# Sorting grouped edge quads in halves of 256, with on-chip copies that bring the rows together again

## The chip, the cores and the metric

The kernel runs on one core of a Trainium2 chip. The metric is device time in microseconds (us), the median of several runs. A core has five engines that run side by side: TensorE (PE, matmuls), VectorE (DVE), ScalarE (ACT), GpSimd (POOL, here the issuer of scatters to device memory) and SyncE (SP, the issuer of loads, stores and copies). Each engine takes its instructions in order; semaphores tie them together. All transfers run on the same 16 DMA engines.

## The reference

One layer of a graph network: 6250 nodes with 128 features and 200,000 edges, sorted by `dst`. Every edge takes the projected row of its `dst` node, multiplies it by a filter that a small network makes from 20 edge features, and adds the product to the row of its `src` node; `src` is random.

```python
h = jnp.maximum(_layernorm(x, axis=-1), 0.0)                  # passed on as atomic_embedding
idx_i = pair_indices[0]                                       # src
idx_j = pair_indices[1]                                       # dst
x = atomic_embedding @ W_in
W_ij = shifted_softplus(f_ij @ W_f1 + b_f1) @ W_f2 + b_f2
W_ij = W_ij * f_ij_cutoff
x_ij = x[idx_j] * W_ij
out = jax.ops.segment_sum(x_ij, idx_i, num_segments=N_ATOMS)
return shifted_softplus(out @ W_o1 + b_o1) @ W_o2 + b_o2      # the caller adds its x
```

## The kernel before, in words

The edges are cut into 391 quads of 512 (four chunks of 128). The main loop (`for i in range(...)`, with `s1_`, `s2_`, `s3_` stages and the hook points `run(i, ...)`) works on several quads at once, each stage one to four iterations behind the one before. For every quad PE makes the filter (`z` L363, `W` L562) and gathers the node rows (`xg` L554), ACT scales them (`xc` L567), and DVE multiplies (`s2_m`, L577). What remains is the sum into the `src` rows, and there are two ways for it:

- A *listed* quad (200 of the 391 go this way or the plain way at the start) gives its product `s` to POOL, which scatters it in four indirect DMAs of 128 rows (`scatter`, L639) with addition into one of four tables `acc` in device memory. `acc_of` rotates the tables, so a scatter waits until the one before it on the same table has landed.
- A *grouped* quad (`sorted_quads`: 191 quads, every second one from 8 on) is summed on PE. Its `src` nodes fall into 16 groups of 392 (`GN`). `rank_*` gives each of 32 chunks' edges its rank within its group and so a slot; `perm_oh` (L719) builds a one-hot matrix `pm` of 128 edges x 576 slots per chunk; `permute` (L744) multiplies it with the three bfloat16 parts of the product (`pt`, 387 columns with two index columns), four blocks of 128 slots (4 groups x 32 slots each), each the sum over four chunks; `perm_out` (L750, ACT) casts a block into `mst`. Edges beyond a group's 32 slots go to 64 overflow slots, which `over_pe` (L757) sorts for two quads into one block of 128 rows; they are summed and scattered by the `over_*` steps, one scatter for a pair of quads.

Eight grouped quads make a round. Four *units* per round then sum the sorted rows: `unit_oh` (L825, DVE) makes one-hots of the local node number, `unit_pe` (L840) multiplies 32-row bands of `mst` with them (four bands beside each other), and `unit_evac` (L851) adds the result to `accT` on chip. `unit_slots` sets the iterations of the units: from `ULAG` iterations after a round's last quad on, at iterations that `UCLASSES` allows, and `mbufs` counts how many `mst` buffers that takes.

The order is written out by hand: `AT` gives each step its distance in iterations from its quad and its hook point (for example `"p0": (3, "PE2")`), `put` and `at` enter it, `clear` moves it off the iterations that hold units. The order of the code is the order on each engine. SP issues, per pair of quads, three `ft` loads (L345), two `rb` loads (L349), a register load (L351) and four `wn` loads (L356), beside the `sb` loads (L394) and the rewriting of the edge features (`fb` L313, `fsd` L335); each waits for a free buffer and for the SP transfer eight before it to land.

After the loop the three remaining tables are loaded, added to `accT` and passed through the output network.

Of the kernel before, what the change touches and what calls it, by code (L numbers as in the profile page):

```python
# [20 lines left out]
P = 128  # L21
# [3 lines left out]
CAP = 32  # L25
OVC = 64
SLOTS = GRP * CAP + OVC
MP0 = 8
# [3 lines left out]
RKQ = 8  # L32
ULAG = 5
AT = {
# [40 lines left out]
def tile_gnn(ctx: ExitStack, tc: tile.TileContext, x, fB, cT, srcT, srcr, srci, dstr, win_, wf1, wf2, bias, bo1c, wo1,  # L75
# [29 lines left out]
    units = {i for us in uslots for i in us}  # L105
    mbufs = [max(len(qs) + sum(q > qs[-1] and (q + 3 if q + 4 in units else q + 4 + s // 2) <= us[s] for q in mpq) for qs, us in zip(rounds, uslots))
             for s in range(4)]
    splain = [q for q in range(NQ) if q not in mpi]
# [292 lines left out]
    def s1_eq(q):  # L401
        if not plainq(q):
            return
        n = plain[q]
        eq = wk.tile([P, 4, P], F32, tag="eq", name="eq", bufs=2)
# [262 lines left out]

    def before_me(ps_t, src, w, own=False):
        n = src.shape[1]  # L670
        nc.tensor.matmul(ps_t, trib if own else tri, src, start=True, stop=False)
        o = ps_t.rearrange("p (j c) -> p j c", c=4 * w)
        v = src.rearrange("p (j c) -> p j c", c=4 * w)
        for k in range(1, 4):
            nc.tensor.matmul(o[:, :, k * w:], onesb, v[:, :, :(4 - k) * w], start=False, stop=(k == 3))

    def rank_count(r):
        n = rk[r]["n"]
        t = ps.tile([P, 512], F32, tag="B", name="rkp", bufs=4)
        before_me(t[:, :n * GRP], rk[r]["G"].rearrange("p x g -> p (x g)"), GRP, own=True)  # L680
        rk[r]["ps"] = t

    def rank_own(r):
        n = rk[r]["n"]
        rank = wk.tile([P, 4 * RKQ], F32, tag="rank", name="rank", bufs=1)[:, :n]
        nc.vector.tensor_reduce(rank, rk[r]["ps"][:, :n * GRP].rearrange("p (x g) -> p x g", g=GRP), axis=AX.X,  # L686
                                op=ALU.max)
        ov = wk.tile([P, 4 * RKQ], BF16, tag="ov", name="ov", bufs=1)[:, :n]
        nc.vector.tensor_scalar(ov, rank, float(BIG + CAP), None, op0=ALU.is_ge)
        rk[r]["rank"], rk[r]["ov"] = rank, ov  # L690

    def rank_over(r):
        t = ps.tile([P, 512], F32, tag="B", name="rko", bufs=4)
        before_me(t[:, :rk[r]["n"]], rk[r]["ov"], 1)
        rk[r]["po"] = t

    def rank_slot(r):
# [3 lines left out]
        a = wk.tile([P, 4 * RKQ], F32, tag="ra", name="ra", bufs=1)[:, :n]  # L701
        nc.vector.scalar_tensor_tensor(a, rk[r]["cnt"], float(CAP), rk[r]["rank"], op0=ALU.mult, op1=ALU.add)
        t = wk.tile([P, 4 * RKQ], F32, tag="rt", name="rt", bufs=1)
        tn = t[:, :n]
        nc.vector.scalar_tensor_tensor(tn, po, float(BIG + GRP * CAP), a, op0=ALU.add, op1=ALU.subtract)
        nc.vector.tensor_tensor(tn, tn, ov, op=ALU.mult)
# [33 lines left out]

    def permute(q, s):
        t = ps.tile([P, 512], F32, tag="B", name="pq", bufs=4)
        for c in range(4):
            nc.tensor.matmul(t[:, :PW], mp[q]["pm"][:, c, s * P:(s + 1) * P], high(mp[q]["pt"][:, c:c + 1, :PW])[:, 0],  # L744
                             start=(c == 0), stop=(c == 3))
        mp[q]["q", s] = t

    def perm_out(q, s):
        mp[q]["ms", s] = wk.tile([P, MW], BF16, tag=f"ms{s}", name="mst", bufs=mbufs[s])
        nc.scalar.copy(mp[q]["ms", s][:, :PW], mp[q].pop(("q", s))[:, :PW])  # L750

    def over_pe(q):
        qs = mpq[mpi[q] // 2 * 2:mpi[q] + 1]
        t = ps.tile([P, 512], F32, tag="B", name="po", bufs=4)
        for c in range(4):
            for h, p in enumerate(qs):
                nc.tensor.matmul(t[h * OVC:(h + 1) * OVC, :PW], mp[p]["pm"][:, c, GRP * CAP:],  # L757
                                 high(mp[p]["pt"][:, c:c + 1, :PW])[:, 0], start=(c == 0), stop=(c == 3))
        mp[q]["po"] = t, len(qs) * OVC

    def over_out(q):
        t, n = mp[q].pop("po")
        mo = mos[mpi[q] // 2 % 2]
        nc.scalar.copy(mo[:n, :PW], t[:n, :PW])
        if n < P:
            nc.vector.memset(mo[n:, :PW], 0.0)

# [52 lines left out]
    def unit_oh(r, s, h):  # L820
        qs = rounds[r]
        for q in qs[h * len(qs) // 3:(h + 1) * len(qs) // 3]:
            so = wk.tile([P, GN], BF16, tag="so", name="so", bufs=RND + 1)
            w = mp[q]["ms", s].bitcast(F32)
            nc.vector.tensor_scalar(so, iotw[:, :GN], w[:, 3 * P // 2:3 * P // 2 + 1], None, op0=ALU.is_equal)  # L825
# [4 lines left out]
    def unit_pe(r, s):  # L830
# [5 lines left out]
        for q in qs:  # L836
            for k in range(3):
                for g in range(4):
                    v = slice(g * CAP, (g + 1) * CAP)
                    nc.tensor.matmul(ts[g][:, :GN], mp[q]["ms", s][v, k * P:(k + 1) * P], mp[q]["oh"][v],  # L840
                                     start=(q == qs[0] and k == 0), stop=(q == qs[-1] and k == 2))
# [53 lines left out]
    with tc.manual_schedule():  # L895
# [266 lines left out]
        def x_load(k):  # L1162
            tag, n = (("pt", 3), ("pt", 3), ("pm", 2), ("pm", 2))[k]
            t_ = pg.tile([P, PW, 4] if tag == "pt" else [P, 4, SLOTS // 2], F32, tag=tag, name="xl")
            v = t_.rearrange("p a b -> p (a b)")
# [98 lines left out]
        for q in mpq:  # L1264
# [135 lines left out]
    with tc.For_i(0, redo, 1):  # L1400
# [8 lines left out]
        with tc.For_i(0, trips, 1) as ci:  # L1409
# [50 lines left out]
            nc.vector.scalar_tensor_tensor(m[:, :P], W, ok[:, 3:4], xw, op0=ALU.mult, op1=ALU.mult)  # L1460
            eq = wk.tile([P, P], F32, tag="eq", name="feq", bufs=2)
            nc.vector.tensor_tensor(eq, sb, scol.to_broadcast([P, P]), op=ALU.is_equal)
# [282 lines left out]
```

## Time and profile before

| | |
|---|---|
| median of 3 runs | 1913.39 us (1912.6 to 1916.29) |
| the profiled execution | 1913.11 us |
| its span, first to last instruction | 1911.3 us |
| mean granted TensorE clock | 0.979 |
| bytes moved by DMA | 267.55 MB in 351575 packets |

How to read the profile: "busy" is the time in which an engine executes; issues of DMAs by SP are not counted as busy. A group row names the line, engine, operation, `out<-in` tiles, shapes and count, then busy us and mean ns of one, then the idle time of the engine just before these instructions and what ended it ("issue" is waiting for nothing that the profile shows). A timeline row has start, length, instruction and, in brackets, the idle time before. PEld is PE's weight load, which overlaps its matmuls; matmuls are pipelined, so their mean length is longer than the busy time each takes.

### The profile page before, as it was taken

The page shows a single profiled execution, that of the slowest core. Times are in us where ns is not written, and L with a number is a line of the kernel's source. Part 1 is how long each engine was busy: PE and PEld are TensorE (multiplying, and loading weights), DVE is VectorE, ACT ScalarE, POOL GpSimd, SP SyncE. Part 2 cuts the span into 40 slices and gives each one's busy share as a digit, 9 for nine tenths or more (in the row PEclk, how much of TensorE's full clock was granted, in tenths as well). Part 3 has the DMA queues.
Part 4 walks back from the last instruction along what each step waited for, and adds up shares of the span by engine and source line. Part 5 has one row for each costly group of instructions (what it writes and reads, how often), then busy time and mean ns, then how long its engine had stood idle before and what let it go on. Part 6 is the DMA issues. An engine that isn't in the chain of part 4 may idle for free. (4 is left out here: it accounts for less than half of the span.)

```text
span 1911.3 us, 58065 instructions
## 1 busy us (share of the span) xinstructions
PE 1809.2 (95%) x20601; PEld 1228.2 (64%) x20601; DVE 1655.9 (87%) x4692; ACT 1474.9 (77%) x4045; POOL 1509.0 (79%) x961
## 2 busy tenths in 40 slices
PE   4679999999999999999999999999999999999986
PEld 3556666666666666666666666666666666666654
DVE  5678998899999989999999889889889888888767
ACT  4569788878887878878887787787787787787725
POOL 4578777788888888887777888888888888878755
PEclk8789999999999999999999999999999999999998
DMA  8788777767776777776776667677676667666648
GB/s 287 201 208 167 142 162 135 131 125 131 139 135 123 131 126 130 129 152 116 125 135 126 124 126 129 118 129 129 116 130 129 116 130 127 117 117 133 106 99 269
DMA packets 351575, 267.55 MB, mean 140 GB/s; under 512 B 96655, under 2 KB 315194, under 8 KB 351282
## 3 DMA queue, kind: packets, MB, share of 16 engines
q1 hardware_dynamic: 218516, 197.56, 35.9%
q0 software_dynamic: 132208, 66.05, 34.6%
q8 instruction: 162, 2.65, 0.6%
q14 instruction: 131, 1.07, 0.2%
q10 hardware_dynamic: 558, 0.20, 0.0%
HBM read 154.65 MB, written 109.00 MB: 138 GB/s over the span
## 5 line engine op out<-in xcount | busy, mean ns | idle before, releaser
L639 POOL DMA_INDIRECT acc<-s,lji x751 | 1201.5, 1600 | 267.9 <-issue 174.4
L744 PE MATMUL pq<-pt,pm 128*128 128x387 bf16 x3056 | 583.2, 337 | 1.2 <-ACT s L597 0.6
L567 ACT ACTIVATE xc<-xg,cb 128x128 f32<-128x128 f32 x1564 | 448.1, 376 | 171.5 <-PE xg L554 151.9
L750 ACT CAST mst<-pq 128x387 bf16<-128x387 f32 x764 | 364.0, 487 | 91.7 <-PE pq L744 68.1
L562 PEld LDWEIGHTS W<-w,a 128*128 128x128 f32 x3128 | 421.7, 196 | 17.9 <-issue 7.3
L744 PEld LDWEIGHTS <-pm 128*128 128x128 bf16 x3056 | 294.4, 98 | 197.5 <-issue 4.9
L840 PE MATMUL un<-so,mst 32*128 32x392 bf16 x9168 | 411.3, 325 | 10.0 <-DVE rank L686 2.8
L562 PE MATMUL W<-w,a 128*128 128x128 f32 x3128 | 420.1, 278 | 0.0
L840 PEld LDWEIGHTS <-mst 32*128 32x128 bf16 x9168 | 249.8, 93 | 146.7 <-issue 19.0
L373 ACT ACTIVATE a<-a,con 128x512 f32<-128x512 f32 x391 | 282.5, 723 | 11.6
L733 DVE TENSOR_TENSOR pt<-pt 128x512 f32<-128x512 f32 x382 | 261.0, 683 | 0.0
L719 DVE TENSOR_SCALAR pm<-iotp,pos 128x576 bf16<-128x576 f16 x764 | 255.6, 396 | 0.0
L368 ACT ACTIVATE a<-z 128x512 f32<-128x512 f32 x391 | 236.6, 605 | 5.9 <-PE z L363 5.9
L851 DVE TENSOR_TENSOR accT<-un,accT 128x392 f32<-128x392 f32 x368 | 182.4, 558 | 63.1 <-PE un L840 34.8
L639 POOL DMA_INDIRECT acc<-os,oji x108 | 180.9, 1675 | 51.3 <-issue 12.9
L825 DVE TENSOR_SCALAR so<-iot,mst 128x392 bf16<-128x392 f16 x764 | 215.3, 333 | 2.2 <-PE un L840 1.9
L577 DVE TENSOR_TENSOR pt<-W,xc 128x512 f32<-128x512 f32 x191 | 131.6, 689 | 57.0 <-ACT xc L567 23.9
L363 PE MATMUL z<-ft,ws 123*128 123x512 bf16 x391 | 153.8, 394 | 19.9 <-POOL b2rep L979 8.4
L554 PE MATMUL xg<-wn,oh 63*128 63x128 bf16 x1564 | 156.6, 221 | 13.5 <-DVE oh L380 12.1
L577 DVE TENSOR_TENSOR s<-W,xc 128x512 f32<-128x512 f32 x188 | 128.7, 685 | 45.5 <-ACT xc L567 34.8
L551 PE MATMUL W<-b2rep,onesb 64*128 64x512 bf16 x391 | 152.9, 391 | 0.0
L639 POOL DMA_INDIRECT acc<-s,ji x48 | 81.0, 1688 | 42.1 <-DMA acc<-s,ji 20.5
(215 smaller groups left out, 1796.0 us busy)
## 6 DMA issues: line engine op xcount, KB each, us to landing
rb<-reld SPq DMA_DIRECT2D x391, 64.0 KB
sb<-src SPq DMA_DIRECT2D x192, 128.0 KB
fsd<-f SPq DMA_DIRECT2D x49, 480.0 KB
ft<-fsd SPq DMA_DIRECT2D x195, 120.0 KB
fb<-in_fB_dram SPq DMA_DIRECT2D x49, 320.0 KB
ft<-fsd SPq DMA_DIRECT2D x195, 80.0 KB
wn<-tab SPq DMA_DIRECT2D x782, 15.8 KB
acc<-s,lji POOLq DMA_INDIRECT x751
```

The source lines that it names most:

```text
L368: nc.scalar.activation(a, st[q]["z"], AF.Exp)
L373: nc.scalar.activation(a, a, AF.Ln, bias=half, scale=0.5)
L562: nc.tensor.matmul(W[:, c, :], st[q]["a"][:, c * P:(c + 1) * P], w2, start=False, stop=(c == 3))
L567: nc.scalar.mul(xc[:, c, :], st[q]["xg"][:, c, :], late["c", q // CQ][:, 4 * (q % CQ) + c:4 * (q % CQ) + c + 1])
L577: nc.vector.tensor_tensor(m[:, :, :P], st[q]["W"], st[q]["xc"], op=ALU.mult)
L639: nc.gpsimd.indirect_dma_start(out=accs[k][:rows, :], out_offset=bass.IndirectOffsetOnAxis(ap=ji, axis=0), in_=s, in_offset=None, compute_ ...
L719: nc.vector.tensor_scalar(pm[:, c], iotp, rk[r]["pos"][:, 4 * j + c:4 * j + c + 1], None, op0=ALU.is_equal)
L733: nc.vector.tensor_tensor(pt[:, :, k * P:(k + 1) * P], a, high(a), op=ALU.subtract)
L744: nc.tensor.matmul(t[:, :PW], mp[q]["pm"][:, c, s * P:(s + 1) * P], high(mp[q]["pt"][:, c:c + 1, :PW])[:, 0], start=(c == 0), stop=(c == 3))
L750: nc.scalar.copy(mp[q]["ms", s][:, :PW], mp[q].pop(("q", s))[:, :PW])
L825: nc.vector.tensor_scalar(so, iotw[:, :GN], w[:, 3 * P // 2:3 * P // 2 + 1], None, op0=ALU.is_equal)
L840: nc.tensor.matmul(ts[g][:, :GN], mp[q]["ms", s][v, k * P:(k + 1) * P], mp[q]["oh"][v], start=(q == qs[0] and k == 0), stop=(q == qs[-1] a ...
```

## The change

A grouped quad is sorted in two halves of 256 edges (two chunks each). A group has 16 slots in a half (`BCAP`) instead of 32 in the quad, so a half fills two blocks of 8 groups x 16 slots, and a block is the sum over two chunks instead of four. ACT casts a half's two blocks into a staging tile `sg`, and two DMAs (`regroup`, issued by SP) copy its 64-partition halves into every second partition of the `mst` tiles, so that the two halves' 16 slots of a group lie together in a band of 32 again. A pair of quads has one overflow block of 128 slots, filled by full-width matmuls, instead of two of 64. The one-hot matrix has 384 columns instead of 576. Units start from 7 iterations after a round's last quad (`ULAG`), not 5; the band-to-group order in `accT` is kept by `unit_evac`. The rank sums count within two chunks, the overflow ranks within eight. `sg` shares the tag of `eq`, which plain quads at the start use, now with 3 buffers.

```diff
 SEG = 512
 GRP = 16
 CAP = 32
-OVC = 64
-SLOTS = GRP * CAP + OVC
+BCAP = 16
+OVC = 128
+SLOTS = GRP * BCAP + OVC
...
-ULAG = 5
+ULAG = 7
 AT = {
...
-    "p2": (4, "PE1"), "p3": (4, "PE1"), "o0": (4, "A0"), "o1": (4, "A0"), "o2": (5, "L"), "o3": (5, "A0"),
+    "p2": (4, "PE1"), "p3": (4, "PE1"), "o0": (4, "A0"), "o1": (4, "A0"), "o2": (5, "L"), "o3": (5, "A0"), "rg0": (4, "A1"), "rg1": (5, "A1"),
...
-    def permute(q, s):
+    def permute(q, k):
+        h, s = divmod(k, 2)
         t = ps.tile([P, 512], F32, tag="B", name="pq", bufs=4)
-        for c in range(4):
+        for c in (2 * h, 2 * h + 1):
             nc.tensor.matmul(t[:, :PW], mp[q]["pm"][:, c, s * P:(s + 1) * P], high(mp[q]["pt"][:, c:c + 1, :PW])[:, 0],
-                             start=(c == 0), stop=(c == 3))
-        mp[q]["q", s] = t
-
-    def perm_out(q, s):
-        mp[q]["ms", s] = wk.tile([P, MW], BF16, tag=f"ms{s}", name="mst", bufs=mbufs[s])
-        nc.scalar.copy(mp[q]["ms", s][:, :PW], mp[q].pop(("q", s))[:, :PW])
+                             start=(c == 2 * h), stop=(c == 2 * h + 1))
+        mp[q]["q", k] = t
+
+    def perm_out(q, k):
+        h, s = divmod(k, 2)
+        if s == 0:
+            mp[q]["sg", h] = wk.tile([P, 2, MW], BF16, tag="eq", name="sg", bufs=3)
+        nc.scalar.copy(mp[q]["sg", h][:, s, :PW], mp[q].pop(("q", k))[:, :PW])
+
+    def regroup(q, h):
+        sg = mp[q].pop(("sg", h))
+        for j in range(2):
+            if h == 0:
+                mp[q]["ms", j] = wk.tile([P, 2, MW], BF16, tag=f"ms{j}", name="mst", bufs=mbufs[j])
+            nc.sync.dma_start(mp[q]["ms", j][h::2, :, :PW], sg[j * HB:(j + 1) * HB, :, :PW])
...
-        for c in range(4):
-            for h, p in enumerate(qs):
-                nc.tensor.matmul(t[h * OVC:(h + 1) * OVC, :PW], mp[p]["pm"][:, c, GRP * CAP:],
-                                 high(mp[p]["pt"][:, c:c + 1, :PW])[:, 0], start=(c == 0), stop=(c == 3))
+        for p in qs:
+            for c in range(4):
+                nc.tensor.matmul(t[:, :PW], mp[p]["pm"][:, c, GRP * BCAP:], high(mp[p]["pt"][:, c:c + 1, :PW])[:, 0],
+                                 start=(p == qs[0] and c == 0), stop=(p == q and c == 3))
...
-                    nc.tensor.matmul(ts[g][:, :GN], mp[q]["ms", s][v, k * P:(k + 1) * P], mp[q]["oh"][v],
+                    nc.tensor.matmul(ts[g][:, :GN], mp[q]["ms", s // 2][v, s % 2, k * P:(k + 1) * P], mp[q]["oh"][v],
...
-            o = (4 * s + g) * GN
+            o = (8 * (s % 2) + 4 * (s // 2) + g) * GN
...
+                for h in range(2):
+                    at(q + 4, "L", regroup, q, h)
             else:
...
+                for h in range(2):
+                    put(f"rg{h}", q, regroup, q, h)
```

How the order on SP changes, at two places. The first is the end of one load group and the start of the next, about the middle of the main loop. `DMAHW0` to `DMAHW7` are the eight semaphores of SP's transfers, `PE_49`, `DVE_49` and `Activation_49` those of the engines; `mst<-sg` is the new copy. Before:

```order
L356 DMA wn<-tab 63x128 [waits DMAHW5_49]
L345 DMA ft_122<-fsd 60x1024 [waits DMAHW6_49,PE_49]
L345 DMA ft_122<-fsd 40x1024 [waits DMAHW7_49]
L345 DMA ft_122<-fsd 20x1024 [waits DMAHW0_49]
L349 DMA rb<-reld 64x512 [waits DMAHW1_49,DVE_49]
```

Now, at the same load group:

```order
L357 DMA wn<-tab 63x128 [waits DMAHW1_49]
L769 DMA mst<-sg 64x2x387 [waits DMAHW2_49,PE_49,Activation_49]
L769 DMA mst<-sg 64x2x387 [waits DMAHW3_49]
L769 DMA mst<-sg 64x2x387 [waits DMAHW4_49,Activation_49]
L769 DMA mst<-sg 64x2x387 [waits DMAHW5_49]
L346 DMA ft_122<-fsd 60x1024 [waits DMAHW6_49]
L346 DMA ft_122<-fsd 40x1024 [waits DMAHW7_49]
L346 DMA ft_122<-fsd 20x1024 [waits DMAHW0_49]
```

Four copies stand between the `wn` loads of one group and the `ft` loads of the next: one pair waits for ACT's casts of the first half, one for those of the second, which ACT makes an iteration later. Here the first copy also waits for PE, for a free `mst` buffer.

The second place is where the feature rewriting is issued, a third of the way through. Before, the write `fsd` (which waits for DVE) and the load `fb` stand alone between two load groups:

```order
L356 DMA wn<-tab 63x128 [waits DMAHW5_49]
L335 DMA fsd<-f_11775 128x3x640 [waits DMAHW6_49,DVE_49]
L313 DMA fb<-in_fB_dram 128x640 [waits DMAHW7_49]
L345 DMA ft_122<-fsd 60x1024 [waits DMAHW0_49,PE_49]
L345 DMA ft_122<-fsd 40x1024 [waits DMAHW1_49]
```

Now:

```order
L769 DMA mst<-sg 64x2x387 [waits DMAHW6_49,Activation_49]
L769 DMA mst<-sg 64x2x387 [waits DMAHW7_49]
L336 DMA fsd<-f_11739 128x3x640 [waits DMAHW0_49,DVE_49]
L314 DMA fb<-in_fB_dram 128x640 [waits DMAHW1_49]
L769 DMA mst<-sg 64x2x387 [waits DMAHW2_49,Activation_49]
L769 DMA mst<-sg 64x2x387 [waits DMAHW3_49]
L346 DMA ft_118<-fsd 60x1024 [waits DMAHW4_49,PE_49]
```

The write and the load now stand between the copies of a quad's first half and those of its second; the same block is rewritten one load group later than before, because the iterations with units have moved.

More of the change, by code (lines that the diff above doesn't have):

```diff
@@ L105, in tile_gnn @@
     units = {i for us in uslots for i in us}
-    mbufs = [max(len(qs) + sum(q > qs[-1] and (q + 3 if q + 4 in units else q + 4 + s // 2) <= us[s] for q in mpq) for qs, us in zip(rounds, uslots))
-             for s in range(4)]
+    mbufs = [max(len(qs) + sum(q > qs[-1] and q + 5 <= us[2 * j + 1] for q in mpq) for qs, us in zip(rounds, uslots))
+             for j in range(2)]
     splain = [q for q in range(NQ) if q not in mpi]
@@ L667, in rank_local, with before_me @@
         rk[r]["ext"] = ext
-    def before_me(ps_t, src, w, own=False):
+    def before_me(ps_t, src, w, m, own=False):
         n = src.shape[1]
         nc.tensor.matmul(ps_t, trib if own else tri, src, start=True, stop=False)
[L672 to L675, printed above, removed]
+        parts = []
+        a = n // (m * w) * m * w
+        if a:
+            parts.append((0, a, m))
+        if a < n:
+            parts.append((a, n, (n - a) // w))
+        for a, b, c in parts:
+            o = ps_t[:, a:b].rearrange("p (j c) -> p j c", c=c * w)
+            v = src[:, a:b].rearrange("p (j c) -> p j c", c=c * w)
+            for k in range(1, c):
+                nc.tensor.matmul(o[:, :, k * w:], onesb, v[:, :, :(c - k) * w], start=False,
+                                 stop=(b == n and k == c - 1))
     def rank_count(r):
@@ L688, in rank_own @@
         ov = wk.tile([P, 4 * RKQ], BF16, tag="ov", name="ov", bufs=1)[:, :n]
-        nc.vector.tensor_scalar(ov, rank, float(BIG + CAP), None, op0=ALU.is_ge)
+        nc.vector.tensor_scalar(ov, rank, float(BIG + BCAP), None, op0=ALU.is_ge)
         rk[r]["rank"], rk[r]["ov"] = rank, ov
@@ L693, in rank_over @@
         t = ps.tile([P, 512], F32, tag="B", name="rko", bufs=4)
-        before_me(t[:, :rk[r]["n"]], rk[r]["ov"], 1)
+        before_me(t[:, :rk[r]["n"]], rk[r]["ov"], 1, 8)
         rk[r]["po"] = t
@@ L701, in rank_slot @@
         a = wk.tile([P, 4 * RKQ], F32, tag="ra", name="ra", bufs=1)[:, :n]
-        nc.vector.scalar_tensor_tensor(a, rk[r]["cnt"], float(CAP), rk[r]["rank"], op0=ALU.mult, op1=ALU.add)
+        nc.vector.scalar_tensor_tensor(a, rk[r]["cnt"], float(BCAP), rk[r]["rank"], op0=ALU.mult, op1=ALU.add)
         t = wk.tile([P, 4 * RKQ], F32, tag="rt", name="rt", bufs=1)
         tn = t[:, :n]
-        nc.vector.scalar_tensor_tensor(tn, po, float(BIG + GRP * CAP), a, op0=ALU.add, op1=ALU.subtract)
+        nc.vector.scalar_tensor_tensor(tn, po, float(BIG + GRP * BCAP), a, op0=ALU.add, op1=ALU.subtract)
         nc.vector.tensor_tensor(tn, tn, ov, op=ALU.mult)
```

18 lines of the change are left out of this document (7 added, 11 removed).

## The prediction

> **What bounds the kernel now.** I read the page's busy line first, then the busy time by stage, then the scatters one by one on the timeline, then the groups and waits. One loop iteration handles one quad; a grouped and a listed quad alternate, so I count in pairs of iterations.
>
> ```profile
> PE 1809.2 (95%) x20601; PEld 1228.2 (64%) x20601; DVE 1655.9 (87%) x4692; ACT 1474.9 (77%) x4045; POOL 1509.0 (79%) x961
> ```
>
> By stage (columns: length, then busy time and instructions of PE, PEld, DVE, ACT, POOL, then clock, DMA share, GB/s):
>
> ```profile
> 200.00:400.00 200.00, 196.57 (x2317) 132.81 (x2316) 182.09 (x524) 162.55 (x452) 158.72 (x100) 1.00 0.73 140
> 400.00:800.00 400.00, 391.87 (x4562) 265.90 (x4564) 367.25 (x1082) 325.13 (x907) 335.96 (x211) 1.00 0.72 131
> 1200.00:1600.00 400.00, 397.33 (x4722) 267.27 (x4711) 352.23 (x975) 322.92 (x883) 332.74 (x205) 1.00 0.69 124
> sum 1550.00, PE 1528.48 PEld 1031.12 DVE 1392.11 ACT 1259.55 POOL 1271.48; mean PE 305.70 PEld 206.22 DVE 278.42 ACT 251.91 POOL 254.30
> ```
>
> PE is busy 1528 of 1550 us: it looks like the only bound, and POOL's 82% looks harmless. The timeline of POOL says otherwise:
>
> ```profile
> 1006.73 1.54 POOL L639 DMA_INDIRECT acc<-s,lji  x1 [0.30 <-DMA acc<-s,lji]
> 1008.57 1.54 POOL L639 DMA_INDIRECT acc<-s,lji  x1 [0.30 <-issue]
> 1010.42 1.56 POOL L639 DMA_INDIRECT acc<-os,oji  x1 [0.30 <-ACT mst L750]
> ```
>
> A scatter shows 1.54 us busy and 0.30 us between it and the next, even when nothing holds it: 1.84 us of POOL. At 400 to 800 us POOL is therefore taken for 335.96 + 211 x 0.30 = 399 of 400 us, at 1200 to 1600 for 394. PE and POOL are both full. How much POOL still waits is read from its groups and from the scatters' first and last start:
>
> ```profile
> L639 POOL DMA_INDIRECT acc<-s,lji x751 | 1201.5, 1600 | 267.9 <-issue 174.4 <-DVE s L577 33.4 <-DMA acc<-s,lji 28.0
> L639 POOL DMA_INDIRECT acc<-os,oji x108 | 180.9, 1675 | 51.3 <-issue 12.9 <-DMA acc<-s,lji 9.7 <-ACT oji L814 9.4
> ...
> L639 POOL DMA_INDIRECT acc<-s,lji x751: 1538/1540/2159, 157.7 to 1840.7; - x188
> L639 POOL DMA_INDIRECT acc<-os,oji x108: 1538/1550/2055, 174.6 to 1857.5; - x108
> ```
>
> From 157.7 to 1857.5 us stand 859 scatters. Busy 1201.5 + 180.9 = 1382, idle before them 267.9 + 51.3 = 319, of which 859 x 0.30 = 258 is the fixed gap. Only 61 us is true waiting. The change keeps all 859 scatters, so POOL caps what any relief of PE can give.
>
> **The change part by part.** Rows for PE, ACT and DVE:
>
> ```profile
> L744 PE MATMUL pq<-pt,pm 128*128 128x387 bf16 x3056 | 583.2, 337 | 1.2 <-ACT s L597 0.6 <-ACT mst L750 0.6
> L757 PE MATMUL po<-pt,pm 128*64 128x387 bf16 x764 | 86.6, 344 | 7.7 <-DVE accT L851 4.0 <-DVE so L825 1.7 <-issue 1.0
> L719 DVE TENSOR_SCALAR pm<-iotp,pos 128x576 bf16<-128x576 f16 x764 | 255.6, 396 | 0.0
> L825 DVE TENSOR_SCALAR so<-iot,mst 128x392 bf16<-128x392 f16 x764 | 215.3, 333 | 2.2 <-PE un L840 1.9 <-issue 0.3
> ```
>
> Sorting matmuls: each of four blocks sums two chunks, not four, so 1528 go, at 583.2/3056 = 0.191 us: 292 us of PE. Overflow matmuls stay 764 but are 128 columns wide. The 64-column ones cost 86.6/764 = 0.113 us each; at the price of the sorting matmuls, whose shape they now have, they cost 0.191: 60 us back. Net 232 us, 1.22 us a pair. The rank matmuls lose and gain 48 and 96 small ones, about 8 us each way.
>
> One-hot builds: 384 columns instead of 576. Between the rows for 576 (0.335 us of busy time) and 392 (0.282 us) the slope gives 0.279, so 764 x 0.055 = 42 us of DVE. ACT's casts keep count and size.
>
> The new copies: 764, issued by SP. No row shows an on-chip copy, so I bound it by SP's nearest issues. First what SP does when nothing holds it, then single issues (min/median/max ns):
>
> ```profile
> 1050.64 1.76 SPq L356 DMA_DIRECT2D wn<-tab  x4
> 1052.51 1.09 SPq L345 DMA_DIRECT2D ft<-fsd  x3
> 1053.69 1.11 SPq L349 DMA_DIRECT2D rb<-reld  x2
> 1055.87 1.76 SPq L356 DMA_DIRECT2D wn<-tab  x4
> ...
> L335 SPq DMA_DIRECT2D fsd<-f x49: 135/417/626, 8.8 to 1749.3; - x49
> L349 SPq DMA_DIRECT2D rb<-reld x391: 465/552/2132, 14.1 to 1800.1; - x196
> L394 SPq DMA_DIRECT2D sb<-src x196: 218/432/2450, 18.1 to 1649.0; - x196
> ```
>
> One load group takes SP 1055.87 - 1050.64 = 5.2 us, once a pair. The gap from one group to the next (1052.51 + 1.09 to 1053.69) is 0.09 us. With one sb load a pair (0.52) and the fsd write and fb load every fourth pair (0.1 each) SP needs about 6.0. Four copies at 0.42 (fsd, nearest in form) to 0.55 (rb, also 64 partitions), plus the gap, add 2.0 to 2.6: 8.0 to 8.6 us a pair, and I take 8.1.
>
> The engines' side: 764 x 128 = 97,800 packets of 774 bytes.
>
> ```profile
> q1 hardware_dynamic: 218516, 197.56, 35.9%
> ```
>
> That is 50 ns a packet of 904 bytes on the mean, so 43 ns by bytes to 50 ns by count: (4.2 to 4.9 ms)/16 engines = 1.4 to 1.6 us a pair. The DMA share is 0.70 over the stages, 6.3 of 9.0 us, and becomes 7.8. It stays below the cap. [...]
>
> SP is one queue: behind a copy that waits for ACT stand the next ft, rb and wn loads, and twice a round a copy waits for PE too, until a unit has freed an mst buffer. The loads are for quads four iterations ahead, so an iteration of delay is covered. If that cover goes, PE waits at L363 and L554 for every pair. The sorted rows now arrive a copy later, but the first unit of a round starts two iterations later and its last one-hots keep two iterations of margin. In the tail the same shift adds one landing, between 0 and the 5.1 us that a table load takes there; I take 3.
>
> The sum, per pair: POOL has 859/188 = 4.57 scatters at (1382/859) + 0.30 = 1.91 us, 8.7 us. The present pair is (1857.5 - 157.7)/188 = 9.0. PE falls from about 8.9 to 7.7, DVE from 8.1 to 7.9, DMA is 7.8, SP 8.1. What is late next is POOL, with SP close behind. Of the 61 us that POOL waits, the last four scatters' share stays, since it waits for the final overflow chain:
>
> ```profile
> 1843.00 1.54 POOL L639 DMA_INDIRECT acc<-os,oji  x1 [0.65 <-DMA acc<-s,lji]
> 1848.17 1.54 POOL L639 DMA_INDIRECT acc<-os,oji  x1 [3.63 <-ACT oji L814]
> 1855.20 2.02 POOL L639 DMA_INDIRECT acc<-os,oji  x1 [5.50 <-ACT oji L814]
> ```
>
> That is about 9, leaving 52. POOL never reaches 100% beside a queue nearly as full, so I take 44. Span 1911.3 - 44 + 3 = 1870; the profiled execution took 1913.1, 1.8 beyond its span and 0.3 under the median of 1913.4. Forecast: 1872 us.
>
> **Rivals.**
>
> *Scatters become shorter.* Many show more than 1.54 us. One such, with what DVE did beside it:
>
> ```profile
> 402.25 0.69 DVE L733 TENSOR_TENSOR pt<-pt 128x512 f32<-128x512 f32 x1
> 402.49 1.88 POOL L639 DMA_INDIRECT acc<-s,lji  x1 [0.30 <-DMA wn<-tab]
> 402.85 0.82 DVE L334 TENSOR_TENSOR f<-fr,f 128x640 bf16<-128x640 f32 x1
> ...
> 1009.64 1.20 DVE L719 TENSOR_SCALAR pm<-iotp,pos 128x576 bf16<-128x576 f16 x4
> ```
>
> If the one-hot builds stretch scatters, the 42 us that they lose come off POOL too: 1872 - 42 = 1830. But beside the four builds at 1009.64 the scatters at 1008.57 and 1010.42 show 1.54 and 1.56; the stretched one lies beside two-input operations, which stay. [...] Chance 0.10.
>
> *SP becomes the bound: slower.* The second copy of a quad waits for a cast of the next iteration, and ACT itself waits for PE in bursts, most after a unit:
>
> ```profile
> ACT xc L567 <- PE xg L554: 151.9, 87, 4.6
> ```
>
> If SP inherits this, 151.9/188 = 0.8 us a pair, on top of the dear 8.6, a pair takes 9.4: 188 x 0.4 = 75 us more, 1990. It decides once SP needs over 9.0 a pair. Against it: the rows below show SP waiting 2.9 us at a time for a wn buffer, so it is ahead of need today. Chance 0.17.
>
> ```profile
> SPq L356 <- PE z L363: 269.2, 92, 6.3
> POOL acc L639 <- DMA acc<-s,lji: 37.7, 78, 3.0
> ```
>
> *The DMA engines answer late.* A scatter waits until the one before it on the same table has landed: 37.7 us now, at a share of 0.70. At 7.8 of 8.7 us, 0.90, waits that double give the gain back: 1872 + 38 = 1910, and more than double is slower. Chance 0.20: 0.08 faster by a little, 0.07 the same, 0.05 slower.
>
> *The change does not fit.* If a pair of quads overflows 128 slots, a flag starts the repair loop of 1563 chunks, and at one scatter of 1.9 us each that alone is 3 ms. Counted in the drawn src, the 96 pairs hold 97 overflowing edges on the mean, and 128 at most: just full. Chance 0.01.
>
> The whole relief of PE, 1911 - 232 = 1680, is excluded: 859 scatters at 1.84 need 1581 us after 157.7, and 54 us of tail follow: not under 1790.
>
> **How the numbers follow.** The forecast, POOL full, has 0.52. Faster (by over 0.2%, about what a measurement of this kernel tells from no change): 0.52 + 0.10 + 0.08 = 0.70. The same: 0.07. Slower: 0.05 + 0.17 + 0.01 = 0.23. The low end is the shorter scatters, 1830; the high end, 1940, takes in the late landings and a third of SP's rival; about 0.05 and 0.12 are left out.
>
> **What would show it.** Right: POOL busy plus 0.30 a scatter at 98% or more from 200 us on, its wait for s gone, PE near 87%, 1528 pq matmuls, a pair at 8.7 to 8.8 us, copies issued in 0.42 to 0.55 us. Wrong: PE waiting for ft or wn, DVE's so waiting for the copies, POOL's wait for acc landings above 75 us, a scatter's mean away from 1.61 us, or SP's issues without gaps while POOL has some.

## The result: 2085.49 us, slower by 9 per cent, and the profile after

| | before | after |
|---|---|---|
| median | 1914.51 us (4 runs, 1912.6 to 1916.29) | 2085.49 us (4 runs, 2079.34 to 2093.25) |
| ratio | | 1.0895, 95% interval 1.0857 to 1.0934 |
| span of the profiled execution | 1911.3 us | 2083.2 us |
| mean granted clock | 0.979 | 0.927 |

The forecast of 1872 us, and its range to 1940, were wrong. First the page of the changed kernel: the line of busy times and the queue of SP's transfers.

```profile
PE 1754.6 (84%) x19124; PEld 1187.4 (57%) x19124; DVE 1600.9 (77%) x4691; ACT 1451.6 (70%) x4045; POOL 1510.1 (72%) x961
q1 hardware_dynamic: 328532, 273.30, 47.5%
```

Busy time by stage (columns as in the prediction):

```profile
400.00:800.00 400.00, 350.96 (x3939) 234.12 (x3938) 328.63 (x1005) 295.76 (x838) 297.72 (x184) 0.94 0.79 159
1200.00:1600.00 400.00, 349.85 (x4032) 235.98 (x4031) 314.25 (x914) 295.18 (x820) 303.29 (x188) 0.95 0.79 155
```

No engine in these columns is full any more. PE fell from 392 to 351 us of 400, but POOL fell too, from 336 to 298: with 184 gaps of 0.30 it is taken for 353 of 400 us, where 399 were expected. Something that the columns do not show sets the pace. The scatters' row (count, then min/median/max ns, first and last start) gives the length of a pair:

```profile
L640 POOL DMA_INDIRECT acc<-s,lji x751: 1538/1541/2488, 159.0 to 2003.2; - x188
```

(2003.2 - 159.0)/188 = 9.81 us a pair; before, by the same row, it was (1840.7 - 157.7)/188 = 8.95. SP's timeline points at the reason (start, length, instructions):

```profile
1044.88 1.82 SPq L357 DMA_DIRECT2D wn<-tab  x4
1046.76 2.68 SPq L769 DMA_DIRECT2D mst<-sg  x4
1049.56 1.28 SPq L346 DMA_DIRECT2D ft<-fsd  x3
1051.26 1.17 SPq L350 DMA_DIRECT2D rb<-reld  x2
1053.48 1.78 SPq L357 DMA_DIRECT2D wn<-tab  x4
```

From one `wn` group to the next SP now takes 1053.48 - 1044.88 = 8.6 us, where it was 5.2, and the four copies are 2.68 of that. (The 1.05 us between the `rb` and the `wn` loads hold the register load, which the timeline leaves out; it was 1.07 before.) One group is a small sample, so I add up all rows of SP's own wait list from 400 to 1600 us: 340.4 us before and 72.6 now, in which SP issued the `rb` loads of 132 and of 121 pairs. The time in which it does not wait it is taken: (1200 - 340.4)/132 = 6.5 us a pair before, (1200 - 72.6)/121 = 9.3 now, 94% of its time. The four copies of a pair add 2.8 us. Over the whole run the first two rows of the list (total, times, longest) are:

```profile
SPq L769 <- ACT sg L762: 31.2, 42, 8.4
SPq L769 <- ACT xc L568: 9.5, 20, 0.9
```

Before, its first row was 269.2 us for `wn` buffers: SP was ahead of need. Now it hardly ever is. The engines' wait list does not say so. Its largest real waits name ACT and the copies:

```profile
ACT sg L762 <- DMA mst<-sg: 226.3, 86, 9.6
DVE s L578 <- ACT xc L568: 221.0, 85, 5.9
POOL acc L640 <- ACT pt L748: 148.8, 61, 8.5
POOL acc L640 <- DMA acc<-s,lji: 24.8, 57, 2.4
```

ACT waits for a staging tile whose copy stands in SP's queue, ACT's later steps stand behind it, and DVE and POOL behind those. From this list two theories follow. The *SP theory*: issuing fills SP, and all else is its echo. The *staging theory*: three staging tiles are too few, and ACT's wait is the cost. A third, the *bytes theory*, blames the 76 MB more on the DMA engines. The lower granted clock (0.927 for 0.979) does not order the times: at 0.949 and 0.948 two of the versions below take 2081.92 us (idle copies) and 1906.58 us (two copies a quad).

### The profile page after: what moved, and what is told of

It is laid out like the page before. It is cut to its first block, busy times and chain, and to the rows that moved or that the text cites. A ratio compares the mean times of both kernels' runs of the same rounds, so it can differ in the third digit from the quotient of the medians.

```text
span 2083.2 us, 56598 instructions
## 1 busy us (share of the span) xinstructions
PE 1754.6 (84%) x19124; PEld 1187.4 (57%) x19124; DVE 1600.9 (77%) x4691; ACT 1451.6 (70%) x4045; POOL 1510.1 (72%) x961
## 3 DMA queue, kind: packets, MB, share of 16 engines
q1 hardware_dynamic: 328532, 273.30, 47.5%
## 5 line engine op out<-in xcount | busy, mean ns | idle before, releaser
L855 PE MATMUL un<-so,mst 32*128 32x392 bf16 x9168 | 515.2, 363 | 112.5 <-ACT sg L762 95.3
L762 ACT CAST sg<-pq 128x387 bf16<-128x387 f32 x764 | 346.8, 493 | 256.5 <-DMA mst<-sg 226.3
L855 PEld LDWEIGHTS <-mst 32*128 32x128 bf16 x9168 | 294.9, 102 | 308.1 <-issue 158.5
L563 PEld LDWEIGHTS W<-w,a 128*128 128x128 f32 x3128 | 432.4, 200 | 59.3 <-issue 46.0
L563 PE MATMUL W<-w,a 128*128 128x128 f32 x3128 | 431.6, 283 | 0.0
L754 PE MATMUL pq<-pt,pm 128*128 128x387 bf16 x1528 | 328.1, 338 | 37.5 <-ACT os L820 12.0
L754 PEld LDWEIGHTS <-pm 128*128 128x128 bf16 x1528 | 145.2, 98 | 145.1 <-issue 55.4
L728 DVE TENSOR_SCALAR pm<-iotp,pos 128x384 bf16<-128x384 f16 x764 | 201.4, 324 | 0.0
L776 PE MATMUL po<-pt,pm 128*128 128x387 bf16 x764 | 153.2, 343 | 0.7 <-issue 0.7
## 6 DMA issues: line engine op xcount, KB each, us to landing
mst<-sg SPq DMA_DIRECT2D x764, 96.8 KB
```

Of the source, the lines that this page charges most:

```text
L563: nc.tensor.matmul(W[:, c, :], st[q]["a"][:, c * P:(c + 1) * P], w2, start=False, stop=(c == 3))
L728: nc.vector.tensor_scalar(pm[:, c], iotp, rk[r]["pos"][:, 4 * j + c:4 * j + c + 1], None, op0=ALU.is_equal)
L762: nc.scalar.copy(mp[q]["sg", h][:, s, :PW], mp[q].pop(("q", k))[:, :PW])
L855: nc.tensor.matmul(ts[g][:, :GN], mp[q]["ms", s // 2][v, s % 2, k * P:(k + 1) * P], mp[q]["oh"][v], start=(q == qs[0] and k == 0), stop=(q ...
```

## The experiments

### The copies taken away, and added to the old kernel

**No copies.** ACT casts straight into `mst` tiles, so the rows of the two halves are not brought together and the sums run over wrong bands; number and shape of all other instructions stay. (The tag of `eq` is back at 2 buffers, and `mst` has one more.)

```diff
-            mp[q]["sg", h] = wk.tile([P, 2, MW], BF16, tag="eq", name="sg", bufs=3)
+            mp[q]["ms", h] = wk.tile([P, 2, MW], BF16, tag=f"ms{h}", name="mst", bufs=mbufs[h])
-            nc.sync.dma_start(mp[q]["ms", j][h::2, :, :PW], sg[j * HB:(j + 1) * HB, :, :PW])
```

> The casts write straight into the mst tiles and the copies are gone (the rows of the two halves are not brought together, so the sums are taken over wrong bands; the number and shape of all other instructions stay). It shows what the relief of PE alone is worth. POOL cap as predicted: 1872 us, between 1850 and 1890, POOL busy plus 0.30 a scatter at 98% or more. If PE's relief is worth all its 232 us: 1680. If something else in the new order costs (later units, wider overflow block): above 1913.

Measured: 1878.56 us, ratio 0.9807 (0.9728 to 0.9886). Its stages, scatters and SP's longest wait:

```profile
400.00:800.00 400.00, 372.51 (x4438) 254.07 (x4438) 363.44 (x1096) 333.56 (x948) 336.90 (x208) 0.98 0.73 135
1200.00:1600.00 400.00, 368.34 (x4476) 249.05 (x4467) 345.55 (x1006) 327.62 (x914) 336.89 (x208) 0.99 0.71 129
```

```profile
L640 POOL DMA_INDIRECT acc<-s,lji x751: 1538/1541/2968, 158.4 to 1810.9; - x188
```

```profile
SPq L357 <- PE z L364: 140.9, 55, 5.1
```

POOL is taken for 336.9 + 208 x 0.30 = 399 of 400 us, a pair takes (1810.9 - 158.4)/188 = 8.79 us, and SP waits for need again. Only two runs were made, at 1872.7 and 1884.43 us. So the cap of the scatters was foreseen rightly, and the copies with all that hangs on them cost 2085 - 1879 = 207 us, give or take 6.

**Idle copies in the old kernel.** The kernel before, plus 764 copies that nothing reads and nothing waits for.

```diff
+    def regroup(q, h):
+        for j in range(2):
+            nc.sync.dma_start(msx[j][h::2, :, :PW], sgx[j * HB:(j + 1) * HB, :, :PW])
+            for h in range(2):
+                at(q + 4 + h, "A1", regroup, q, h)
```

> The kernel before, unchanged, with 764 copies of the change's shape added on SP (from one staging tile to two others; nothing reads them, nothing waits for them). SP theory: the copies fill SP's queue (6.0 us of issuing a pair before, plus 2.7 or more for four copies and the drift of its neighbours, against a pair of 9.0), so the loads come late although TensorE, VectorE and ScalarE do exactly what they did: 1990 to 2090 us, SP without gaps. Staging theory (the wait for a staging buffer is what costs): 1914, since no one waits for these copies. Engine theory (it is the 128-wide matmuls and the ranking that cost): 1914 too.

Measured: 2081.92 us, ratio 1.0868 (1.0849 to 1.0886). Its copies, and the first row of SP's wait list:

```profile
L759 SPq DMA_DIRECT2D msx<-sgx x764: 590/633/2437, 116.7 to 1990.9; - x191
```

```profile
SPq L350 <- PE pq L749: 13.8, 30, 1.1
```

Copies alone make nearly the whole loss, with no one waiting for them and with every other instruction of the loop as before. That settles it against the staging theory. They also do not wait for ACT here, and all rows of SP's wait list over the run, those for landed transfers among them, add up to 184.5 us, where the kernel before has 566.6. So it is not SP's waiting either: it is their issue.

**The same, 16 columns wide.** As above with `:16` in place of `:PW`: 32 bytes a row and block instead of 774, and by the page 4.0 KB a copy instead of 96.8.

> As the kernel before with 764 idle copies on SP, but 16 columns wide: the same number of instructions and of packets, 32 bytes a packet where the change has 774. Issue theory (what counts is how long SP needs to issue a copy): the same time as with full copies, within 15 us. Bytes theory (the DMA engines are crowded by 74 MB more): 1914 to 1930 us.

Measured: 2061.91 us, ratio 1.0787 (1.0769 to 1.0805).

```profile
L759 SPq DMA_DIRECT2D msx<-sgx x764: 590/632/1810, 116.2 to 1962.4; - x191
```

The median issue is 632 ns against 633. Of the 167 us only 20 go with the bytes; 147 stay.

### More staging

```diff
-            mp[q]["sg", h] = wk.tile([P, 2, MW], BF16, tag="eq", name="sg", bufs=3)
+            mp[q]["sg", h] = wk.tile([P, 2, MW], BF16, tag="eq", name="sg", bufs=4)
```

> Four staging tiles instead of three (there is no room for more). SP theory: SP is full at 9.7 us a pair whatever the buffers are, so 2085 within 1%, the wait of the casts only moves. Staging theory: the 226 us of waiting for a staging tile shrink by a third or more and the time falls to 2010 or less. Bytes theory: 2085.

Measured: 2102.59 us, ratio 1.0977 (1.0936 to 1.1018). From its wait list:

```profile
POOL acc L640 <- ACT pt L748: 140.3, 32, 11.3
ACT os L533 <- PE lsum L528: 115.9, 11, 13.4
...
ACT sg L762 <- DMA mst<-sg: 59.2, 38, 8.0
```

The wait that headed the list falls from 226.3 to 59.2 us, and the time does not fall at all; the waiting appears elsewhere. The largest row named a victim. (Two runs; 2102.59 us lies within the 1 per cent that the SP theory gave.)

### The copies on another queue

**All on ACT:** `nc.scalar.dma_start` in place of `nc.sync.dma_start`.

> All 764 copies are issued by ACT instead of SP. If SP's issue time is the cause (SP theory): SP falls back to about 6 of 10 us a pair and waits again for PE, the casts no longer wait 226 us for the staging tile, and the time depends on whether an issue keeps ACT's datapath: about 1880 us if it does not, about 1950 if each takes 0.6 us of ACT (1452 + 764 x 0.63 = 1930 us of ACT). If the 16 DMA engines are the cause (bytes theory): the same bytes, so 2085 within 1%. If three staging tiles are too few (staging theory): the copies start as soon as the casts are done, so it also falls, to about 1880.

Measured: 2300.0 us, ratio 1.2007 (1.1932 to 1.2083). The copies in ACT's queue, and the first rows of the wait list:

```profile
L769 ACTq DMA_DIRECT2D mst<-sg x764: 597/605/2017, 98.0 to 2218.2; - x191
```

```profile
DVE s L578 <- ACT xc L568: 403.9, 141, 6.1
POOL acc L640 <- ACT pt L748: 248.0, 55, 7.2
ACT a L369 <- DMA mst<-sg: 194.9, 55, 5.6
```

**Every second one on ACT:**

```diff
-            nc.sync.dma_start(mp[q]["ms", j][h::2, :, :PW], ...)
+            (nc.scalar if j else nc.sync).dma_start(mp[q]["ms", j][h::2, :, :PW], ...)
```

> Of the two copies of a half one is issued by SP and one by ACT. SP theory: SP needs 9.7 - 1.3 = 8.4 us a pair, below POOL's 8.7, and ACT 1452 + 382 x 0.63 = 1690 us: about 1880 us. Bytes theory: 2085 within 1%. Staging theory: little change, since one of the two copies still waits in SP's queue: 2050 or more.

Measured: 2100.45 us, ratio 1.0966 (1.0918 to 1.1013).

Both runs missed what the theories had given: no forecast for the first was above 2085 us, and the SP theory had about 1880 for the second. SP was relieved as meant: in the first run its queue (q1 hardware_dynamic) carries 218516 packets, as in the kernel before, where the change has 328532. But an issue costs 0.605 us on ACT too, and there it is taken from an engine with work: 764 x 0.605 = 462 us for all, 231 for half. With its busy time ACT is then taken for 1464.5 + 462 = 1927 of 2303 us. That is not full, so the sum alone does not give the time; ACT also waits 194.9 us in the row of the copies above, and DVE and POOL wait for ACT's steps. That what SP saved is paid by ACT is argued from these rows; how much of the loss each makes stays open. So moving the issues does not show what relief is worth; they have to become fewer.

### Relief for SP that costs no other engine

**Contiguous copies.** Three lasting staging tiles (the tag of `eq` is back at 2 buffers), whole rows: one run of 1552 bytes a partition in place of two of 774. By the count of SP's queue a copy has (279636 - 218516)/764 = 80 packets; in the change it has (328532 - 218516)/764 = 144.

```diff
-            nc.sync.dma_start(mp[q]["ms", j][h::2, :, :PW], sg[j * HB:(j + 1) * HB, :, :PW])
+            nc.sync.dma_start(mp[q]["ms", j][h::2], sg[j * HB:(j + 1) * HB])
```

> The change with three lasting staging tiles whose rows are copied whole (1552 bytes in one run a partition, in place of two runs of 774), so each copy has half the packets. Issue theory, if a copy's issue goes by its packets (0.63 us for 128 of them): 0.35 to 0.45 us a copy, SP saves about 1 us a pair, 195 pairs, so 1880 to 1930 us. If the issue goes by partitions or bytes, it stays at 2085. Staging theory: 2085.

Measured: 2026.67 us, ratio 1.059 (1.0563 to 1.0618).

```profile
L775 SPq DMA_DIRECT2D mst<-sg x764: 461/587/2217, 117.9 to 1947.0; - x191
```

The issue fell only from 627 to 587 ns, where 0.35 to 0.45 us were expected: it does not go by packets. 764 x 0.04 = 31 us of the 59 follow from it; the rest is not accounted for.

**One `rb` load a pair.**

```diff
-        for j in range(nh):
-            nc.sync.dma_start(rb[j * HB:(j + 1) * HB], reld[s:s + 1, j * SEG:(j + 1) * SEG].to_broadcast([HB, SEG]))
+        nc.sync.dma_start(rb[:nh * HB], bass.AP(tensor=reld.tensor, offset=..., ap=[[SEG, nh], [0, HB], [1, SEG]]))
```

> The change with the two row loads of a pair (rb, 64 partitions each) in one instruction of the same bytes. SP theory: if one load for 128 partitions is issued in 0.6 us as each of the two is now, SP saves 0.5 to 0.6 us a pair, some 100 to 115 us: 1970 to 1990. If its issue goes by the rows it writes, 1.1 us, nothing is saved: 2085. Staging theory and bytes theory: 2085 either way, since no buffer and no byte changes.

Measured: 2075.99 us, ratio 1.0832 (1.0808 to 1.0856): 9 us where 100 were expected. SP's wait list has rows that the change does not have:

```profile
SPq L769 <- DMA rb<-reld: 42.4, 59, 2.2
...
SPq L336 <- DMA rb<-reld: 24.3, 19, 2.3
SPq L314 <- DMA rb<-reld: 13.7, 15, 1.8
```

Every SP transfer waits for the one eight before it to land (the semaphores DMAHW0 to DMAHW7 of the order above), and this load, though issued in 0.578 us as hoped, now lands so late that SP stands still for 80 us in these three rows. Most of the saved issue time was spent on that. What makes it land late was not shown.

**One `ft` load, with contiguous copies.** The DRAM table keeps six parts for three, so a pair's features come in one load; 49 blocks are stored in three pieces.

```diff
-    fsd = dp.tile([NB, 3, RB * BE], BF16, name="fsd")
+    fsd = dp.tile([NB, 6, RB * BE], BF16, name="fsd")
-        for g, m in FPARTS:
-            nc.sync.dma_start(ft[g * RB:(g + m) * RB, :n], fsd[b, :m]...)
+        nc.sync.dma_start(ft[:6 * RB, :n], fsd[b].rearrange("g (r e) -> (g r) e", r=RB)[:, o:o + n])
```

> The change with contiguous copies (as before, 2027 us) and the three loads of a pair's features (ft) in one: the table in DRAM holds each part as often as it is loaded (six rows for three, so 23.5 MB more are written, by two more stores for each of 49 blocks). SP theory: per pair 1.3 us of issues become 0.6, 98 stores of 0.55 us are added, net 80 us less on SP: 1930 to 1960. DMA traffic theory (the engines are crowded by bytes): 2027 or somewhat more, as bytes are added. Staging theory: 2027.

Measured: 1988.3 us, ratio 1.0368 (1.034 to 1.0396): 38 us less than with contiguous copies alone, half of what was expected, with 24 MB more written.

**And `rb` for two pairs at once** (64 partitions still, two rows of 1024 bytes each; for room, the tiles `os` have 5 buffers instead of 6):

```diff
+        if s % 2 == 0:
+            for j in range(2):
+                nc.sync.dma_start(rbs[0][j * HB:(j + 1) * HB, :m], reld[s:s + m, ...].unsqueeze(0).to_broadcast([HB, m, SEG]))
```

> As the one with contiguous copies and one ft load, and the row loads (rb) of two pairs taken at once: two instructions for four quads in place of four, each with twice the bytes. SP theory: 0.58 us a pair less again, 110 us; then SP needs less than the scatters do, and the cap of the scatters shows: 1878 to 1900, faster than before. If the larger loads land late and later issues wait for them, as in the run with one rb load for 128 partitions, 1920 to 1960. DMA traffic theory: 2027 or more.

Measured: 1911.44 us, ratio 0.9991 (0.9971 to 1.0011): 77 us less again, and the whole loss is gone.

**Both loads, but the change's own copies:**

> The change itself, copies as they are, with the one ft load and the rb loads of two pairs at once. SP theory: 2085 less 80 less 110: 1890 to 1920. DMA traffic theory: 2085 or more.

Measured: 1943.12 us, ratio 1.0133 (1.0111 to 1.0154). 142 us of the 171 come back although no copy, no staging tile and no byte of the copies was touched, and more bytes move.

**The control: the old kernel with the one `ft` load:**

> A control: the kernel before with the one ft load alone. Its SP had gaps in a quarter of the time, so by the SP theory relief there is worth nothing: 1905 to 1917. If the one load itself moved the time by another way (bytes, landing), it would show here.

Measured: 1913.9 us, ratio 0.9996 (0.9987 to 1.0006). Where SP has gaps, the same edit is worth nothing.

### What makes a copy dear

**No stride at the destination:** `[h * HB:(h + 1) * HB]` in place of `[h::2]`, so the bands hold wrong rows.

> The change with each copy written to 64 neighbouring rows in place of every second row (the bands then hold wrong rows; instructions, packets and bytes are the same). If the stride of the destination is what makes a copy's issue 0.63 us, it falls to 0.3 or 0.4 and the time to 1890 to 1950. If not, 2085 as the change.

Measured: 2096.11 us, ratio 1.0945 (1.0925 to 1.0965).

**Half as many copies, each of 128 rows** (here too the bands hold wrong rows)**:**

```diff
-        for j in range(2):
-            nc.sync.dma_start(mp[q]["ms", j][h::2, :, :PW], sg[j * HB:(j + 1) * HB, :, :PW])
+        nc.sync.dma_start(mp[q]["ms", h][:, :, :PW], sg[:, :, :PW])
```

> The change with one copy of 128 rows for each half in place of two of 64 (the bands then hold wrong rows; 382 instructions, packets and bytes the same). If the cost is by instruction, 0.6 to 0.75 us a copy, SP saves some 200 us and the cap of the scatters shows: 1880 to 1910. If it goes by packets, 1.26 us a copy, nothing is saved: 2085.

Measured: 1910.76 us, ratio 0.9982 (0.9968 to 0.9996). The copies of the two, in this order:

```profile
L769 SPq DMA_DIRECT2D mst<-sg x764: 156/627/1769, 115.8 to 2012.2; - x191
```

```profile
L767 SPq DMA_DIRECT2D mst<-sg x382: 356/667/1702, 117.1 to 1826.1; - x191
```

The stride does nothing: 627 ns with and without. Twice the rows a copy cost 0.04 us more, and half the instructions give back 175 us. The price is by instruction.

### What is left when SP has room

**The version at 1911 us, and two `sb` loads in one:**

```diff
+        if len(qs) == 2 and qs[1] == qs[0] + 2:
+            nc.sync.dma_start(t_.rearrange("p (j e) -> p j e", j=2),
+                              src16[q // 2:q // 2 + 2, o:o + SEG].unsqueeze(0).to_broadcast([P, 2, SEG]))
```

> The run with contiguous copies, one ft load and rb loads of two pairs (1911, SP still without gaps), and the index loads (sb) of two ungrouped quads in one instruction in place of two, the bytes the same. SP theory: 96 issues of 0.55 us less, some 50 us: 1865 by SP alone, so the cap of the scatters shows, as without copies: 1878 to 1895, faster than before. If the copies have another price of their own (staging, DMA engines) that SP's has hidden: 1900 to 1912. If the larger load lands late: 1905 to 1915.

Measured: 1908.41 us, ratio 0.9965 (0.9951 to 0.9979): hardly less, though SP has 95 issues fewer. That speaks for another price beside SP's.

**Two copies a quad, the right rows.** The staging tile holds both halves; one copy fills one destination. (`os` has 4 buffers here and in the next two.)

```diff
-            nc.sync.dma_start(mp[q]["ms", j][h::2], sg[j * HB:(j + 1) * HB])
+            nc.sync.dma_start(mp[q]["ms", j].rearrange("p s w -> p (s w)"),
+                              sg[j * HB:(j + 1) * HB].rearrange("p h s w -> p h (s w)"))
```

> The change with the right rows but two copies a quad in place of four: staging for both halves in one tile, and one copy of 64 rows by two halves for each of the two destinations (382 instructions, 128 packets of 1552 bytes each). Issue theory: 0.6 to 0.7 us a copy, SP saves 1.2 us a pair against four contiguous copies, so as the run with half the copies or a little better: 1885 to 1910. If the issue goes by packets: 1.2 us, 2027 as the contiguous one. If the later copy (after both halves) makes the units late: 1930 or more.

Measured: 1906.58 us, ratio 0.9957 (0.9944 to 0.997).

```profile
L776 SPq DMA_DIRECT2D mst<-sg x382: 523/597/2244, 117.6 to 1824.9; - x191
```

**The same, with one `ft` load and one `sb` load:**

> As the one with two copies a quad, with the one ft load and the merged sb load as well. SP theory: SP needs about 7.5 us a pair against 8.7 of the scatters, so its gaps come back and the scatters set the time: 1872 to 1890, faster than before by 1.5 to 2 per cent. If the copies or the added writes have a price of their own beside SP's: 1895 to 1910 with gaps on SP.

Measured: 1914.74 us, ratio 1.0003 (0.9993 to 1.0013). **The same, with the `sb` load alone:**

> Two copies a quad (1907 us, SP 97% full, DMA engines 0.85 busy) and the merged sb load, which adds no byte: SP gets 96 issues of 0.54 us less, 50 us. If SP still held the run with two copies a quad: 1880 to 1895. If the DMA engines' late landings hold it (POOL waited 85 us in all for landed scatters there, 55 without copies): 1900 to 1910.

Measured: 1898.63 us, ratio 0.9913 (0.9894 to 0.9932), the fastest of the versions that keep the right rows, and 0.9 per cent faster than before. First the run with `ft` and `sb`: SP's first wait, a stage, and POOL's waits for landings.

```profile
SPq L342 <- DVE f L340: 74.9, 35, 4.4
```

```profile
400.00:800.00 400.00, 364.80 (x4316) 247.59 (x4316) 356.24 (x1085) 323.50 (x918) 335.38 (x208) 0.97 0.89 189
```

```profile
POOL acc L649 <- DMA acc<-s,lji: 53.7, 96, 2.5
POOL acc L649 <- DMA acc<-s,ji: 30.9, 15, 4.3
```

The same stage and waits of the run with `sb` alone:

```profile
400.00:800.00 400.00, 366.92 (x4352) 249.36 (x4351) 360.96 (x1096) 325.79 (x926) 335.68 (x209) 0.98 0.86 177
```

```profile
POOL acc L650 <- DMA acc<-s,lji: 38.1, 76, 2.5
POOL acc L650 <- DMA acc<-s,ji: 26.5, 17, 4.6
```

And the run without copies:

```profile
POOL acc L640 <- DMA acc<-s,lji: 27.3, 65, 1.5
POOL acc L640 <- DMA acc<-s,ji: 20.5, 13, 4.3
```

In this stage POOL is at its cap in all three, taken for 398 to 399 of 400 us, so what sets them apart lies mostly outside it: from 157 to 400 us the run without copies has 120 POOL instructions, the one with `ft` and `sb` 115. The sum of the two landing waits goes 47.8, 64.6, 84.6 us, steps of 17 and 20. The profiled executions took 1884.43, 1896.76 and 1914.24 us, steps of 12 and 17, and the DMA share goes 0.73, 0.86, 0.89. It would fit a price that SP had hidden: scatters that land later when the DMA engines carry more. But the version at 1911 us with two `sb` loads in one, profiled at 1898.73 us, does not fit so simple a rule:

```profile
400.00:800.00 400.00, 366.11 (x4328) 248.21 (x4328) 358.66 (x1089) 325.06 (x922) 336.52 (x208) 0.99 0.89 189
```

```profile
POOL acc L654 <- DMA acc<-s,lji: 34.8, 77, 1.7
POOL acc L654 <- DMA acc<-s,ji: 20.1, 16, 3.8
```

Its DMA share is 0.89 too, and its landing waits are 54.9 us, less than at 0.86. So the share alone does not set the landing waits, no run took landing time away by itself. With `ft` and `sb` it is not SP either, which waits for DVE's `f` again (74.9 us). What the copies still cost once SP has room, some 20 us from 1878.6 to 1898.6, stays open.

## Why the prediction was wrong, point by point

**SP's sum: the step that failed.** "Four copies at 0.42 (fsd, nearest in form) to 0.55 (rb, also 64 partitions), plus the gap, add 2.0 to 2.6: 8.0 to 8.6 us a pair, and I take 8.1." Two terms of it were too small. The median issue of a copy was 0.627 us, above both ends, and by the wait lists the four add 2.8 us a pair, not 2.1. And without copies SP needs 6.5 us a pair, not "about 6.0": the group that was timed was a quiet one, and the `lm`, `tab`, `xt` and `cb` loads are not in the sum. Rows from the same part of the old kernel's timeline, beside the 1.11 us of `rb` in that group:

```profile
1047.69 1.88 SPq L349 DMA_DIRECT2D rb<-reld  x2
1057.73 1.79 SPq L508 DMA_DIRECT2D lm<-acc  x4
1060.86 1.30 SPq L349 DMA_DIRECT2D rb<-reld  x2
```

Together 9.3 us in place of 8.1, above POOL's 8.7, so SP and not POOL set the time. One error alone would have left SP level with POOL: 6.5 + 2.1 = 8.6, 6.0 + 2.8 = 8.8. It took both to meet the prediction's own condition, "once SP needs over 9.0 a pair".

**The rival "SP becomes the bound".** The right resource, but 95 us short of the time (1990, chance 0.17), and with the wrong mechanism: not ACT's bursts, for which SP's copies waited 31.2 us in its largest row, but the issues themselves, as the idle copies in the old kernel show.

**"An iteration of delay is covered."** It is, for a delay. A queue that needs 9.3 us of work for each 9.0 us pair falls behind with every pair, and no lead helps: after some pairs the whole loop runs at SP's pace (9.81 us a pair measured). An issue of 0.63 us, four times a pair, was enough here to fill SP.

**POOL's cap.** Right: 1872 forecast, 1878.6 without copies, 8.7 to 8.8 us a pair forecast and 8.79 measured there. The sign named for it (POOL busy plus its gaps at 98% or more) holds there, and the other named sign, SP's issues without gaps while POOL has some, holds in the change.

**PE and DVE.** The rows of the changed kernel's groups:

```profile
L754 PE MATMUL pq<-pt,pm 128*128 128x387 bf16 x1528 | 328.1, 338 | 37.5 <-ACT os L820 12.0 <-issue 4.5 <-ACT sg L762 3.4
L776 PE MATMUL po<-pt,pm 128*128 128x387 bf16 x764 | 153.2, 343 | 0.7 <-issue 0.7
L728 DVE TENSOR_SCALAR pm<-iotp,pos 128x384 bf16<-128x384 f16 x764 | 201.4, 324 | 0.0
L640 POOL DMA_INDIRECT acc<-s,lji x751 | 1212.6, 1615 | 285.9 <-issue 178.7 <-DVE s L578 65.8 <-DMA acc<-s,lji 19.4
```

A sorting matmul costs 328.1/1528 = 0.215 us, not 0.191, an overflow one 0.200: PE lost 188 us of these, not 232. Its busy time as a whole fell by only 55 us, from 1809.2 to 1754.6, for the units' matmuls (L855) show 515.2 us where they showed 411.3; without the copies they show 407.3, and why they grow in the change was not tried. A pair takes 351 x 9.81/400 = 8.6 us of PE, not 7.7; that PE is busy for 88% of the stage, near the 87% named as a sign, is luck. The one-hot builds lost 54 us, not 42. None of this sets the time: neither engine is full.

**Shorter scatters.** No: 1.615 us on the mean against 1.600, with smaller one-hot builds (201.4 us of DVE against 255.6). What makes some scatters show 1.88 us in place of 1.54 was not tried.

**The DMA engines' share.** 7.8 us a pair forecast from the packets' mean, 0.79 x 9.81 = 7.7 measured.

**Late landings.** Not in the change, whose scatters come more rarely (24.8 us against 37.7). Once SP is relieved, one run with the share of 0.89 has 53.7 us in this row and 1914.7 us, near the 1910 given for it; but the version with the same share above has 34.8 us, so the rival's mechanism is not shown.

## What to carry to other kernels

A queue that issues transfers is an engine with a capacity (here 9.3 us of issues met a pair of 9.0): add its instructions up at their measured issue times, over many periods and not from one quiet group, all loads and gaps included, and compare the sum with the period, also when the page does not count it as busy. When the wait list points everywhere, add the suspected work, idle, to the old kernel, or take it away: two runs said here what the largest wait of the list did not. What relieved the queue here was fewer instructions that each carry more: 382 copies for 764 took the time from 2085 to 1911 us. It did not where they landed late: one `rb` load for two left SP waiting 80 us and brought 9. Moved to ACT, which had work, an issue cost 0.605 us there, where it cost 0.627 on SP.

## What the runs showed of the hardware that was not expected

- In these runs a copy on chip held its issuing queue for about 0.6 us almost whatever it carried: 0.632 us on the median with 4.0 KB and 0.633 with 96.8; 0.587 with 80 packets, 0.667 with 272 ((322420 - 218516)/382); 0.627 with and without a row stride; 0.605 on ACT's queue. Steps of this size say little of packets or rows: SP's half of the change's own copies, when every second one went to ACT, had a median of 0.654, and two copies a quad have 0.597 with 144 packets.
- Two `rb` loads of 64 partitions joined into one of 128 were issued in 0.578 us, and SP then waited 80 us for their landing, so that almost nothing was gained (2076.0 against 2085.5 us). The same bytes joined along the row for two pairs brought 77 us (1988.3 to 1911.4).
- A sorting matmul summed over two chunks instead of four costs 0.215 us instead of 0.191, in the run without copies too (327.8 us in all there), where the granted clock was 0.963. What makes it so was not tried.
